# Layer 0's loop on one Trainium2 core: ScalarE copies the taps ahead of statistics and k, and GpSimd makes the differences of x one unit sooner, in three pieces around its ticks

## The chip, the cores and the metric

The kernel runs on one core of a Trainium2 chip. The metric is the device time of one launch in microseconds. TensorE (PE) multiplies matrices, VectorE (DVE) and ScalarE (ACT) work on tiles in SBUF and PSUM, GpSimd (POOL) on tiles in SBUF, and SyncE (SP) issues the DMAs. Each engine works through its own list of instructions in order, and this kernel writes that order out by hand.

## The reference, cut to what matters

The input x is 4 x 64 x 256 x 256 in float32. Layer 0 adds to x a convolutional block of its group norm, and layer 1 adds to that a block of two 3x3 convolutions with batch norms. The change is in layer 0:

```python
h = gelu(conv2d(gn(x), c1_w, 3x3) + c1_b)
h = c1x1(h, c2_w, c2_b)
xa, k = split(h, 2)
xs = conv2d(xa, sh_w, 1x3, groups=C) + sh_b      # the taps, across
xs = gelu(conv2d(xs, sv_w, 3x1, groups=C) + sv_b) # the taps, down
pooled = xs.mean(axis=(2, 3))                     # gate: weights of 3 experts
for (w1, w2, w3) in experts:
    out += mask * c1x1(c1x1(k, w2) * c1x1(xs, w1), w3)
x = x + c1x1(out, proj_w, proj_b)
```

## The kernel before, in words

**Units and slots.** Layer 0 cuts the four images into 64 units of 16 rows each (two halves of 8 rows on the two halves of the 128 partitions). `plan_front` (from L1023) lays the work of all units into slots. In slot u the engines do, side by side, the 3x3 convolution of unit u, the preparation of units u+1 and u+2, and the taps of units u-1 and u-2. `at_slot(u, pos, call)` puts a call at a position in the slot; positions run from 0 to about 9.2. All calls are sorted by slot and position and then issued under a manual schedule, so a position decides where the instructions of a call stand in each engine's own queue and nothing else: a call at 4.3 and one at 4.5 run at the same time if they are on different engines and no data binds them.

**The convolution** is done in a transformed domain along the rows (six products in place of the rows' taps). What goes into it is the tile `v` with six parts, of which there is one copy. GpSimd makes it out of a unit's ten rows, tile `x`:

- `x_four` (L522, ScalarE, one instruction at L526): four times some rows, into `x4`. One buffer.
- `x_differences` (L528, GpSimd, six instructions): two that finish `x4` (L532), then four that turn x in place into differences two rows apart (L535), each of which waits for the one before. `x_edges` (L510) puts the mean in place of a row beyond the image at the first and last unit of an image, one more instruction (L517), seven times in all.
- `x_scaled` (L537, ScalarE): twice some rows of the differences into `e2` (L540), and four times others in place (L542). It needs all the differences.
- `v_inner` (L551, GpSimd): v1 and v2 from x4 (L556, L557), v3 and v4 from the differences and e2 (L558, L559).
- `v_outer` (L561, GpSimd): v0 and v5 from the scaled differences (L563, L564).

TensorE reads v in `front_conv` (matmuls at L492): v1 and v2 at position 1, v3 and v4 at 1.3, v0 and v5 at 5. Each part of v can be written for unit u+1 only when these matmuls of unit u are through. ScalarE copies one half of each result (`front_copy`, tile `mc`, L594), VectorE combines them in PSUM (L599 to L618), and ScalarE takes the gelu into `h` (`front_h`, L626).

**The taps.** `front_taps_a` opens the one PSUM bank `ps_a` for one half of a unit's rows (24 records of 64x512); `front_taps_b` adds the rows at the edges (eight records of 64x256). Then ScalarE copies the bank, scaled, into t (`front_taps_i`, L666), VectorE adds the left and the right neighbour out of the bank (`front_taps_h`, L672 and L675, then L678 on t alone), and ScalarE takes the gelu into xs (`front_xs`, L694). The bank is free for the next half when L675 has read it. Each slot has two such halves: of unit u-2 at positions 2, 4, 4.15, 5.2, 5.3, and of unit u-1 at 7, 9, 9.1 and, in the slot after, 1.15 and 1.55.

**Ticks.** Between `front_taps_a` and `front_taps_b` stands `divide` (L483): GpSimd sets one column (`tick`, L485) when the last matmul issued before it is through, and the first matmul of the edge taps waits for that instruction. There are two in each slot, at 2.2 and 7.2. A tick is an instruction in GpSimd's queue like any other.

**What else ScalarE does.** `stats_piece` (L426, tile `xs_in`, L432) sums x plus a shift and then its squares for the next image's group norm, two instructions a piece. The plan gives slots 1 to 11 three pieces each (two in slot 11) and slots 12 to 43 two; slots 44 to 63 have none. In even slots `front_k` (L701) multiplies h with the experts' matrix for k into the bank `p` (L708), and ScalarE copies it (L716); in odd slots `front_q` and `front_low` do the like with xs, with VectorE reading the result.

**Output work** of an earlier image joins the loop from slot 19 on: TensorE's `ps_o` at positions 3 and 6 in the bank `p`, VectorE's L831 and L836, loads and stores on SP. The group norms' and the gate's small steps sit at fixed places, some with a table load on ScalarE ahead of `front_xs`.

After slot 63 the loop's last steps are put among the steps of layer 1 by a table (`TAIL`).

## Time and profile before

| What | us |
|---|---|
| Median of three runs | 3071.86 (3065.21 to 3072.45) |
| The profiled execution | 3069.24 |
| Its span, first to last instruction | 3067.4 |
| Busy: PE, DVE, ACT, POOL | 2372.5, 2458.7, 2054.9, 1675.0 |
| Granted TensorE clock, mean | 0.911 |

| Stretch of the loop, us | PE busy | DVE busy | ACT busy | POOL busy | DMA share |
|---|---|---|---|---|---|
| 97 to 467 | 316.14 | 260.12 | 312.89 | 294.62 | 0.61 |
| 467 to 928 | 421.27 | 377.24 | 342.45 | 337.45 | 0.94 |
| 928 to 1305 | 361.02 | 333.40 | 222.51 | 291.31 | 0.87 |

The profile shows one execution. A group's row gives the line, engine, operation and tiles (out <- in), and how often and how long it ran. A row of the timeline gives the start, the duration, the engine and line, and, in brackets, how long the engine had been idle before and what released it. A row of the waits gives the total, the number and the longest. TensorE's weight loads (PEld) are listed apart from its matmuls. The loop of layer 0 fills the first 43% or so of the span; layer 1's convolutions and the last pass over the output fill the rest.

### The profile page before, as it was taken

To read this page: it belongs to the slowest core of one execution; us is meant where nothing else is said; L and a number is where in the kernel's file an instruction comes from. 1 tells how busy PE (TensorE), PEld (TensorE's weight loads), DVE (VectorE), ACT (ScalarE), POOL (GpSimd) and SP (SyncE) were. 2 spreads that over 40 slices of the span, in tenths; PEclk is the share of its full clock that TensorE was granted. 3 is DMA by queue.
4 is the path that set the end of the run, shared out by engine and by line. 5 is a ranking of instruction groups with operands and counts; after the bars stand their busy time and mean duration, and the time that the engine had idled before them with its cause. 6 is when DMAs were issued, how large, how long until landed. Compare 5 with 4: busy or idle time off the path is not lost.

```text
span 3067.4 us, 53128 instructions
## 1 busy us (share of the span) xinstructions
PE 2372.5 (77%) x21576; PEld 1519.2 (50%) x21576; DVE 2458.7 (80%) x2793; ACT 2054.9 (67%) x2274; POOL 1675.0 (55%) x1210
## 2 busy tenths in 40 slices
PE   1888889998999999978889999998999999200000
PEld 1444445444444545545566666776888888200000
DVE  5567677888888988867788888988998999886665
ACT  6888877777776655556566767877888888433222
POOL 5877877777677877744345545645555555000000
PEclk9999999999999999999999999998999999655555
DMA  8664579999898989838889988765777764799999
GB/s 339 205 226 188 193 254 338 344 352 327 323 348 297 307 290 315 301 146 294 320 303 343 362 316 326 261 250 195 262 265 260 271 255 142 305 426 427 426 427 405
DMA packets 135573, 915.36 MB, mean 298 GB/s; under 512 B 14944, under 2 KB 15712, under 8 KB 40608
## 3 DMA queue, kind: packets, MB, share of 16 engines
q1 hardware_dynamic: 135328, 911.97, 79.6%
q8 instruction: 169, 2.77, 0.4%
q14 instruction: 76, 0.62, 0.1%
HBM read 573.74 MB, written 338.17 MB: 297 GB/s over the span
## 4 chain that ended last, share of the span: by engine, by line
PE 27%; DMA 18%; DVE 6%; issue 2%; ACT 1%; POOL 1%; SPq 0%; DVEq 0%; ACTq 0%; POOLq 0%
PE ps_h L295 17%; PE ps_h2m L295 6%; DMA y_end<-y_d 5%; DMA h<-h_d 4%; DMA out<-h 3%; DMA y<-in_xp 3%; PE ps_hm L295 3%; DMA xs_in<-xs_d 2%; DVE h L317 1%; PE ps_o L492 1%; DVE diff L352 1%; DVE odd L361 1%; DMA yn<-y_d 1%; DVE y L831 1%; DVE h L1398 1%
## 5 line engine op out<-in xcount | busy, mean ns | idle before, releaser
L295 PE MATMUL ps_h<-diff,w_q 128*128 128x512 f32 x3072 | 754.6, 400 | 11.5 <-DVE h L317 11.5
L295 PEld LDWEIGHTS ps_h<-diff,w_q 128*128 128x128 f32 x3072 | 579.2, 190 | 183.7 <-issue 29.9
L492 PE MATMUL ps_c<-v,us 64*64 64x256 f32 x9216 | 541.2, 383 | 37.4 <-DVE ps_c L612 32.7
L342 POOL TENSOR_TENSOR d<-yn 128x1024 f32<-128x1024 f32 x128 | 355.9, 2801 | 319.1 <-DMA yn<-y_d 182.1
L492 PE MATMUL ps_a<-h,av 64*64 64x512 f32 x4080 | 400.5, 506 | 88.6 <-DVE t L675 69.2
L492 PEld LDWEIGHTS ps_c<-v,us 64*64 64x64 f32 x9216 | 362.9, 135 | 189.0 <-DVE ps_c L612 40.7
L342 POOL TENSOR_TENSOR d<-h 128x1024 f32<-128x1024 f32 x127 | 312.1, 2480 | 194.6 <-DVE diff L350 133.4
L317 DVE SCALAR_TENSOR_TENSOR h<-ps_h,scale_w,m 128x1024 f32<-128x1024 f32 x256 | 323.5, 1279 | 63.5 <-PE ps_h L295 47.3
L492 PEld LDWEIGHTS ps_a<-h,av 64*64 64x64 f32 x4080 | 160.3, 136 | 369.4 <-issue 260.6
L535 POOL TENSOR_TENSOR x<-x 128x512 f32<-128x512 f32 x256 | 328.2, 1282 | 15.5
L672 DVE SCALAR_TENSOR_TENSOR t<-ps_a,m,t 128x1020 f32<-128x1020 f32 x128 | 163.6, 1278 | 201.4 <-ACT t L666 200.7
L1397 ACT ACTIVATE v<-y_end,shift,gn 128x2048 f32<-128x2048 f32 x64 | 133.8, 2092 | 279.2 <-DMA y_end<-y_d 244.0
L381 ACT ACTIVATE junk<-h,less_h 128x2048 bf16<-128x2048 f32 (+3 forms) x133 | 256.0, 1925 | 11.1 <-DVE h L317 10.9
L1398 DVE SCALAR_TENSOR_TENSOR h<-h,ss,v 128x2048 f32<-128x2048 f32 x64 | 149.8, 2350 | 120.2 <-ACT v L1397 120.2
L831 DVE SCALAR_TENSOR_TENSOR y<-ps_o,ob,y 128x1024 f32<-128x1024 f32 x128 | 163.9, 1280 | 90.6 <-PE ps_o L492 43.1
L666 ACT ACTIVATE t<-ps_a,tap_bias,m 128x1024 f32<-128x1024 f32 x128 | 153.8, 1201 | 99.3 <-PE ps_a L492 98.8
L295 PE MATMUL ps_h2m<-odd,w_q 128*128 128x512 f32 x768 | 193.2, 400 | 8.2 <-DVE odd L361 4.4
L694 ACT ACTIVATE xs<-t 128x1024 f32<-128x1024 f32 x128 | 134.5, 1051 | 94.0 <-issue 72.7
L295 PE MATMUL ps_hm<-odd,w_q 128*128 128x512 f32 x768 | 194.2, 402 | 3.7 <-DVE t L675 3.0
L352 DVE SCALAR_TENSOR_TENSOR diff<-d,gn,diff 128x1024 fp32r<-128x1024 f32 x128 | 190.3, 1517 | 4.9 <-ACT diff L345 4.9
L345 ACT ACTIVATE diff<-d 128x1024 fp32r<-128x1024 f32 x128 | 135.1, 1055 | 83.6 <-POOL d L342 82.3
L626 ACT ACTIVATE h<-ps_c,c1b 128x1024 f32<-128x1024 f32 x128 | 135.6, 1110 | 73.3 <-DVE ps_c L618 69.7
(226 smaller groups left out, 4348.0 us busy)
## 6 DMA issues: line engine op xcount, KB each, us to landing
h_d<-h SPq DMA_DIRECT2D x114, 1024.0 KB
x<-in_xc SPq DMA_DIRECT2D x64, 1280.0 KB
h<-h_d SPq DMA_DIRECT2D x64, 1152.0 KB
yn<-y_d SPq DMA_DIRECT2D x60, 1152.0 KB
xs_in<-in_xp SPq DMA_DIRECT2D x64, 1024.0 KB
xs_d<-xs SPq DMA_DIRECT2D x128, 512.0 KB
xs_in<-xs_d SPq DMA_DIRECT2D x64, 1024.0 KB
y<-in_xp SPq DMA_DIRECT2D x64, 1024.0 KB
```

The costliest lines, as they stand in the source:

```text
L295: nc.tensor.matmul(ps, wq[w][:, kind, kx, :], t[:, rows, kx : kx + W], start=(j == 0), stop=(j == len(terms) - 1))
L317: nc.vector.scalar_tensor_tensor(h.rearrange("p (e k) w -> p e (k w)", e=2), ps.rearrange("p e k w -> p e (k w)"), w_scale[w], m.unsqueeze ...
L342: engine.tensor_tensor(raw.rearrange("p (g r) w -> p g r w", g=2), *pair, ALU.subtract)
L352: nc.vector.scalar_tensor_tensor(lower, raw, scale, upper.bitcast(F32), ALU.mult, ALU.subtract)
L381: nc.scalar.activation(junk[rows, 0:n], flat(h), AF.Square, bias=less[name][rows], accum_out=total)
L492: last[:] = [nc.tensor.matmul(ps[o, at_out[0] : at_out[1], :], w[i], rhs[i], **flags)]
L535: nc.gpsimd.tensor_tensor(x[:, r : r + 2], x[:, r + 2 : r + 4], x[:, r : r + 2], ALU.subtract)
L626: nc.scalar.activation(hs[u][:, :, rows, :], ps, AF.Gelu, bias=c1_bias[u // NCH])
L666: nc.scalar.activation(flat(t), flat(ps), AF.Identity, bias=tap_bias, scale=sh[:, 1:2])
L672: nc.vector.scalar_tensor_tensor(t[:, :, 1:W], ps[:, :, 0 : W - 1], sh[:, 0:1], t[:, :, 1:W], ALU.mult, ALU.add)
L831: nc.vector.scalar_tensor_tensor(y, ps.rearrange("p x s w -> p x (s w)"), out_bias[b], y, ALU.add, ALU.add)
L1398: nc.vector.scalar_tensor_tensor(h, h, ss2[:, 0:1], v, ALU.mult, ALU.add)
```

## The change

ScalarE: the statistics move. Of the pieces in the first half of a slot the sum goes from position 1.12 to 1.6, behind the copies of the convolution, `x_scaled` and `front_xs`; the squares stay at 4.4. Of the pieces in the second half the sum goes from 6.5, behind `front_h`, to 5.4, ahead of it, and the squares from 7.15 to 9.15, behind the copy of the taps (9.1). The copy of k's result leaves `front_k` (position 8) and becomes `front_k_out` at 9.2, also behind the copy of the taps.

GpSimd: `x_differences` is split into `x_fourths` (the two on x4) and `x_seconds` (two of the four on x at a time). In place of all six for unit u+1 at 0.5, behind the second tick of the slot before, stand, for unit u+2: the fourths at 4.5 (behind `x_four` at 4.3, which doesn't move), two of the seconds at 6.6 and two at 7.3, with the second tick (7.2) between. `v_inner` is split too: v1, v2 and v3 at 1.9, ahead of the first tick (2.2), and v4 at 2.3 behind it. Only slot 0 still makes all differences of unit 1 at 0.5. GpSimd's order in a slot is so:

| Before | After |
|---|---|
| fourths, four seconds (u+1) | v1, v2, v3 (u+1) |
| tick one | tick one |
| v1, v2, v3, v4 (u+1) | v4 (u+1) |
| v0, v5 (u+1) | fourths (u+2) |
| tick two | v0, v5 (u+1) |
| | two seconds (u+2) |
| | tick two |
| | two seconds (u+2) |

No arithmetic is added or left out, and no DMA, matmul or VectorE instruction changes its place in its queue.

```diff
+    def x_fourths(u):
+        x4 = x4s[u]
         for j in (1, 2):
             nc.gpsimd.tensor_tensor(x4[:, j - 1], x_rows(u, j + 2), x4[:, j - 1], ALU.subtract)
-        x_edges(u)
-        for r in range(0, 8, 2):
+
+    def x_seconds(u, rows):
+        x = xt[u]
+        if 0 in rows:
+            x_edges(u)
+        for r in rows:
             nc.gpsimd.tensor_tensor(x[:, r : r + 2], x[:, r + 2 : r + 4], x[:, r : r + 2], ALU.subtract)
...
-    def v_inner(u):
+    def v_inner(u, part=None):
+        if part != 1:
...
+            nc.gpsimd.tensor_tensor(at_v(3), x_rows(u, 2), e2s[u], ALU.add)
+        if part != 0:
+            nc.gpsimd.tensor_tensor(at_v(4), x_rows(u, 2), e2s.pop(u), ALU.subtract)
...
+        ps_k[b, j] = ps
...
+    def front_k_out(b, j):
+        ps = ps_k.pop((b, j))
         k_sb[b, j] = work.tile([P, 2, GF], F32, tag="k", name=f"k_{b}_{j}", bufs=1)
         nc.scalar.activation(flat(k_sb[b, j]), ps.rearrange("p s f -> p (s f)"), AF.Identity, bias=k_bias)
...
             if u + 1 <= last:
-                at_slot(u, 0.5, x_differences, u + 1)
+                if u == 0:
+                    at_slot(u, 0.5, x_differences, 1)
                 at_slot(u, 1.5, x_scaled, u + 1)
-                at_slot(u, 2.3, v_inner, u + 1)
+                at_slot(u, 1.9, v_inner, u + 1, 0)
+                at_slot(u, 2.3, v_inner, u + 1, 1)
                 at_slot(u, 5.5, v_outer, u + 1)
             if u + 2 <= last:
                 at_slot(u, 4.3, x_four, u + 2)
+                at_slot(u, 4.5, x_fourths, u + 2)
+                at_slot(u, 6.6, x_seconds, u + 2, (0, 2))
+                at_slot(u, 7.3, x_seconds, u + 2, (4, 6))
...
                 at_slot(u, 8, front_k, *divmod(j, NOCT // 4))
+                at_slot(u, 9.2, front_k_out, *divmod(j, NOCT // 4))
...
-                    at_slot(int(s), ((1.12, 4.4) if first else (6.5, 7.15))[part], stats_piece, b, 2 * k + i, part)
+                    at_slot(int(s), ((1.6, 4.4) if first else (5.4, 9.15))[part], stats_piece, b, 2 * k + i, part)
```

The table `TAIL` gets one more entry, for the copy of k's result in slot 64: (3, 13.35).

## The prediction

> **What bounds the kernel now.** I read the page (busy shares), then the waits of 140 to 1540 us, then the timeline of two slots. The change touches only layer 0's loop: 64 slots, from about 64 to 1340 us, some 20 us each. Its waits (who waited for whom: total us, times, longest):

> ```profile
> POOL tick L485 <- PE ps_a L492: 298.0, 109, 10.0
> DVE t L672 <- ACT t L666: 181.8, 89, 8.6
> PE ps_a L492 <- DVE t L675: 68.8, 41, 7.6
> PEld ps_a L492 <- POOL tick L485: 11.9, 17, 0.8
> ```

> GpSimd mostly waits for TensorE at its ticks and hardly ever the other way round; TensorE's largest wait is for L675, the second reader of the single tap bank. A slot with statistics shows why (start us, duration, engine, line):

> ```profile
> 827.17 0.66 PE L492 MATMUL ps_a<-h,av 64*64 64x256 f32 x8
> 827.92 1.15 ACT L432 ACTIVATE xs_in<-xs_in,shift 128x1024 f32<-128x1024 f32 x1
> 829.19 1.06 ACT L432 ACTIVATE xs_in<-xs_in 128x1024 f32<-128x1024 f32 x1
> 830.24 1.19 ACT L666 ACTIVATE t<-ps_a,tap_bias,m 128x1024 f32<-128x1024 f32 x1
> 832.78 1.28 DVE L675 SCALAR_TENSOR_TENSOR t<-ps_a,m,t 128x1020 f32<-128x1020 f32 x1
> 834.21 2.38 PE L492 MATMUL ps_a<-h,av 64*64 64x512 f32 x24 [1.19 <-ACT e L540]
> 838.09 0.64 PE L492 MATMUL ps_a<-h,av 64*64 64x256 f32 x8
> 838.88 1.21 ACT L666 ACTIVATE t<-ps_a,tap_bias,m 128x1024 f32<-128x1024 f32 x1 [2.54 <-PE ps_a L492]
> 839.98 1.05 ACT L526 ACTIVATE x<-x 128x1024 f32<-128x1024 f32 x1
> ```

> I cut every slot at its two groups of edge taps (the eight 64x256 matmuls on ps_a, each behind a tick): B, position 9, here at 827.17; A, position 4, ending here at 838.73. Read from the timeline, B to the end of A takes 11.56 us in such slots and 12.53 with k; the end of A to the next B takes 8.28. Without statistics TensorE has no gap, and the slot is 18.96:

> ```profile
> 1239.31 0.61 PE L492 MATMUL ps_a<-h,av 64*64 64x256 f32 x8
> 1242.90 1.29 POOL L563 TENSOR_TENSOR v<-x 128x512 f32<-128x512 f32 x1
> 1244.15 1.27 POOL L564 TENSOR_TENSOR v<-x 128x512 f32<-128x512 f32 x1
> 1247.12 0.10 POOL L485 MEMSET tick<- 128x1 f32 x1 [1.70 <-PE ps_a L492]
> 1247.24 2.53 POOL L532 TENSOR_TENSOR x<-x,x 128x512 f32<-128x512 f32 x2
> 1248.78 0.66 PE L492 MATMUL ps_a<-h,av 64*64 64x256 f32 x8
> 1249.72 5.33 POOL L535 TENSOR_TENSOR x<-x 128x512 f32<-128x512 f32 x4
> ```

> The second tick stands right behind v_outer here, so it was ready 1.7 us before TensorE let it go, and all six differences of x ran after it. From B to B the three stretches took: 97.11 to 427.06, 17 slots without output work, 330.0 us; 427.06 to 950.86, 25 with output and statistics, 523.8; 950.86 to 1305.65, 18 with output alone, 354.8. Sum 1208.5.

> [...] the tick starts when its predecessors and PE are done. [...] Here the spans are 1.28, the spacing 1.25 (1242.90 to 1244.15), and 1.35 where one difference waits for the one before ((5.33-1.28)/3). [...] the trace's 1.25 is used. [...] the trace has 1.05 (square) and 1.14 (identity).

> **The change part by part.**

> *ScalarE, position 9.* The statistics pair (2.32 us, 827.92 to 830.24) and k's copy (L716, about 1.0) leave the front of L666. L666 then starts right after B's end, at B+0.8, L675 ends at about B+4.7, and conv's two groups hold TensorE until B+5.7. The wait is gone: B to A falls to 10.14, as in the slots without statistics. Gain 1.42 and 2.39 a slot. Identity at 5.4 fits the gap ahead of gelu (1.51 idle before L626 in such slots). Square and k's copy now end at B+4.1, ahead of the second mc copy (B+5.9): nothing. k's bank is next written by output work at about B+8: nothing.

> *ScalarE, position 1.6.* The identity moves from 1.12 to behind xs. Spacings of the slot at 827.17: mc at B+5.93, e 6.42, x 7.08, xs 8.04, so the identity starts at 9.10 and, with 1.13 each, lets L666 (position 4.15) go at B+10.23 (one) or 11.36 (two, in four early slots). With output work A ends at B+10.14, L666 could go at 10.28 anyway: nothing. Without output work A ends at about B+9.12, and it costs 1.0 or 2.1.

> *GpSimd, first half.* v1 to v3 go ahead of tick one. v1 waits for conv's first group (B+3.3), v3 for e (B+7.05), so tick one is at about B+8.4; TensorE wants it at B+8.2 without output work, a microsecond later with it. Cost 0.2 or nothing.

> *GpSimd, second half: the large term.* Queued ahead of tick two are now: two fourths (L532), waiting for ScalarE's L526, then two v_outer, then two of the four seconds. Behind the tick stands TensorE's B. L526 is behind L666, which waits for A. So, from the end of A: L666 at 0.14, L526 at 1.25 (1.11 later), its end 2.30, fourths 2.36, v_outer 4.84, seconds 7.33, their end 7.33+1.35+1.28 = 9.96, tick and semaphore 0.10: B at A+10.06. Before, 8.28 in most slots and 8.65 to 8.86 in the last ones. Cost 1.2 to 1.8 in every one of 60 slots. The cover was TensorE's own 8.3 us; the chain is longer than that. The latency ScalarE to GpSimd (0.06) is the least known: 0.0 to 0.2. In 7 slots x_edges (L517, 0.92, spacing 0.9) joins this chain.

> *Not moved:* no DMA issue; x's loads keep their place on SP's queue, and v_outer, later by some 2.4 us, still frees the ring tile before the load that takes it (position 0 of the next slot).

> The sum. Period = start of L666 + 9.92.
> Stretch 1: four slots of 11.36+9.92 = 21.28, 85.1; thirteen of 20.15, 262.0; edges 1.8; two slots with table loads ahead of xs (2.9 us of ScalarE at about 338 us), now in the chain, 6: 354.9, against 330.0, +24.9.
> Stretch 2: 25 of 10.14+10.06 = 20.20, 505.0; edges 1.8; three slots with table loads 6; stalls of the gate and of throttled stretches that stay, read as the excess of B to A over 12.5 (4.3 and three of 1.7) 9.4: 522.2, against 523.8, -1.6.
> Stretch 3: 18 of 20.20, 363.6; edges 2.7; table loads 6; stalls that stay 5: 377.3, against 354.8, +22.5.
> Prologue: seconds of unit 2 move ahead of tick one of slot 1: +1.5.
> Total +47. The profiled execution took 3069.24 (span 3067.4), so 3116 on its own time; the median shown is 2.6 higher, and I leave it at 3116, since with TensorE idle more, some of the half-clock stretches in the loop may not come.

> **Rivals.**
> 1. The tick comes free (faster). Then only the removed wait counts: 25 slots of 1.9, 48, and five early ones (B to A 10.9 to 13.6, down to 9.3) 16: 3005. This needs the path from L526's end to tick two to fit in 8.28-2.30 = 6.0 us; six operations at 1.25 are 7.5, and 298 us of waiting at ticks, which speaks for it, lies in places that the new order can't use, since L526 comes late. Against it: that is queue order.
> 2. A wash. The chain as computed, but nothing else: table loads, edges and double identities hidden, stalls gone. 17 of 19.18 and 43 of 20.20 are 1194.7, 14 less than before: at best 3055, with half of the extras 3080. For it: TensorE's new idle time can absorb DVE's delays. Against it: the identity and the table loads are on ScalarE ahead of L666, and the chain has no slack.
> 3. More is late: the identities at 5.4 push gelu beyond B in early slots[...]. 0.2 us on each of six operations is 60 x 1.2 = 72: 3150 and more. The spacings hardly vary in the trace.

> **Chances.** Forecast 0.72 (3090 to 3140), wash 0.15 (3055 to 3090), tick free 0.05, more late 0.08. A measurement can tell about 0.3%, 9 us, from no change. Range 3085 to 3140: the latency's ends are -4 and +8, the kept stalls and table loads (33) may halve or grow by a quarter. Faster 0.06, same 0.09, slower 0.85.

> **What would show it.** After: the waits lose PE ps_a <- DVE L675 and have PE ps_a <- POOL tick as TensorE's largest in the loop, near 1.3 to 1.9 us a slot; GpSimd's wait at the second tick is gone, and it waits for L526 instead; B to A is 10.1 and A to B 10.1 in slots with output, which shows as one period, near 20.2, with and without statistics. It is wrong if B follows A by 8.3, or if L532 starts before L666.

## The result, and the profile after

| What | Before | After |
|---|---|---|
| Median of four runs, us | 3068.53 (3060.53 to 3072.45) | 3145.88 (3144.6 to 3146.63) |
| Ratio, 95% interval | | 1.0255 (1.0231 to 1.0279) |
| Span of the profiled execution | 3067.4 | 3144.3 |
| Mean granted clock | 0.911 | 0.91 |

The change costs 77 us. The forecast had the direction and the mechanism, and +47; its range ended at 3140. In the changed kernel lines above 526 have moved: e is L549, taps copy L677, the two readers L683 and L686, k's copy L733, the seconds L540, the fourths L532.

The waits of the changed kernel, 140 to 1620 us (total us, times, longest):

```profile
DVE t L683 <- ACT t L677: 190.8, 111, 6.6
POOL x L532 <- ACT x L526: 182.9, 58, 5.7
PE ps_a L492 <- POOL tick L485: 105.3, 72, 2.8
PE ps_a L492 <- DVE t L686: 57.2, 25, 7.6
POOL tick L485 <- PE ps_a L492: 41.8, 7, 10.0
```

The third and the last row have changed places against the kernel before: GpSimd's tick hardly ever waits for TensorE now, TensorE waits for the tick 72 times. L686, the second reader of the bank, isn't gone: in rows with statistics and output (440 to 960) TensorE waits 13.3 us for it (27.4 before, 430 to 950), but in the rows without output, ahead of 440, still 30.3 (26.5 before), there between A and B. The POOL row with L526 is new and says what the tick is late for: the fourths wait for it 58 times. One slot shows the chain (start us, duration, engine, line; idle time before in brackets):

```profile
1206.51 0.61 PE L492 MATMUL ps_a<-h,av 64*64 64x256 f32 x8
1207.25 1.21 ACT L677 ACTIVATE t<-ps_a,tap_bias,m 128x1024 f32<-128x1024 f32 x1 [1.10 <-PE ps_a L492]
1208.36 1.05 ACT L526 ACTIVATE x<-x 128x1024 f32<-128x1024 f32 x1
1209.48 2.50 POOL L532 TENSOR_TENSOR x<-x,x 128x512 f32<-128x512 f32 x2 [2.78 <-ACT x L526]
1211.95 1.30 POOL L574 TENSOR_TENSOR v<-x 128x512 f32<-128x512 f32 x1
1213.20 1.28 POOL L575 TENSOR_TENSOR v<-x 128x512 f32<-128x512 f32 x1
1214.43 2.63 POOL L540 TENSOR_TENSOR x<-x 128x512 f32<-128x512 f32 x2
1217.00 0.10 POOL L485 MEMSET tick<- 128x1 f32 x1
1217.16 0.66 PE L492 MATMUL ps_a<-h,av 64*64 64x256 f32 x8 [1.69 <-POOL tick L485]
```

A ends at 1207.12 and B starts at 1217.16, 10.04 later; in between GpSimd runs without a gap from the end of L526 on, and TensorE stands still for 1.69.

From here on a row is the piece of the loop from one B to the next, numbered 1 to 63; rows 1 to 17, 18 to 42 and 43 to 60 are the three stretches of the forecast. Row 1 begins at 100.07 (97.11 before).

| Rows | Before | Forecast | After |
|---|---|---|---|
| 1 to 17 | 330.0 | 354.9 | 364.5 |
| 18 to 42 | 523.8 | 522.2 | 532.5 |
| 43 to 60 | 354.8 | 377.3 | 382.6 |
| 61 to 63 | 65.1 | not forecast | 66.9 |
| Start of row 1 | 97.11 | +1.5 | +2.96 |

A regular row with output is 10.14 + 10.04 = 20.18 (forecast 20.20), one without output 9.20 + 10.88 = 20.08 (20.15), one with two identities 21.20 (21.28). So the chain was right to 0.1 us, and what is missing, 25 us in rows 1 to 60, lies in the irregular rows.

### The profile page after: what moved, and what is told of

The parts are those of the page before. It is cut to its first block, busy times and chain, and to the rows that moved or that the text cites. A ratio compares the mean times of both kernels' runs of the same rounds, so it can differ in the third digit from the quotient of the medians.

```text
span 3144.3 us, 53038 instructions
## 1 busy us (share of the span) xinstructions
PE 2372.0 (75%) x21576; PEld 1507.4 (48%) x21576; DVE 2500.6 (80%) x2793; ACT 2055.5 (65%) x2274; POOL 1667.4 (53%) x1210
## 3 DMA queue, kind: packets, MB, share of 16 engines
q8 instruction: 169, 2.77, 0.4%
## 4 chain that ended last, share of the span: by engine, by line
PE 27%; DMA 18%; DVE 5%; issue 2%; ACT 1%; SPq 0%; POOL 0%; DVEq 0%; ACTq 0%
PE ps_h L295 17%; PE ps_h2m L295 5%; DMA y_end<-y_d 4%; DMA out<-h 4%; DMA h<-h_d 4%; PE ps_hm L295 3%; DMA y<-in_xp 2%; DMA xs_in<-xs_d 2%; PE ps_o L492 1%; DVE h L317 1%; DVE diff L352 1%; DVE odd L361 1%; DVE y L848 1%; DMA y_d<-y 1%; DVE h L1422 0%
## 5 line engine op out<-in xcount | busy, mean ns | idle before, releaser
L492 PE MATMUL ps_c<-v,us 64*64 64x256 f32 x9216 | 547.3, 387 | 22.7 <-DVE ps_c L623 18.3
L492 PE MATMUL ps_a<-h,av 64*64 64x512 f32 x4080 | 399.4, 506 | 173.4 <-POOL tick L485 110.1
L492 PEld LDWEIGHTS ps_c<-v,us 64*64 64x64 f32 x9216 | 364.3, 137 | 176.9 <-DVE ps_c L623 20.7
L492 PEld LDWEIGHTS ps_a<-h,av 64*64 64x64 f32 x4080 | 155.2, 136 | 454.0 <-issue 211.7
L540 POOL TENSOR_TENSOR x<-x 128x512 f32<-128x512 f32 x256 | 328.5, 1283 | 13.3
L683 DVE SCALAR_TENSOR_TENSOR t<-ps_a,m,t 128x1020 f32<-128x1020 f32 x128 | 163.7, 1279 | 213.8 <-ACT t L677 213.8
L532 POOL TENSOR_TENSOR x<-x,x 128x512 f32<-128x512 f32 x128 | 160.4, 1275 | 211.0 <-ACT x L526 211.0
L677 ACT ACTIVATE t<-ps_a,tap_bias,m 128x1024 f32<-128x1024 f32 x128 | 153.9, 1202 | 113.5 <-PE ps_a L492 113.4
```

Of the source, the lines that this page charges most:

```text
L492: last[:] = [nc.tensor.matmul(ps[o, at_out[0] : at_out[1], :], w[i], rhs[i], **flags)]
L532: nc.gpsimd.tensor_tensor(x4[:, j - 1], x_rows(u, j + 2), x4[:, j - 1], ALU.subtract)
L540: nc.gpsimd.tensor_tensor(x[:, r : r + 2], x[:, r + 2 : r + 4], x[:, r : r + 2], ALU.subtract)
L677: nc.scalar.activation(flat(t), flat(ps), AF.Identity, bias=tap_bias, scale=sh[:, 1:2])
L683: nc.vector.scalar_tensor_tensor(t[:, :, 1:W], ps[:, :, 0 : W - 1], sh[:, 0:1], t[:, :, 1:W], ALU.mult, ALU.add)
```

## The experiments

Each is compared with the kernel before, run beside it on the same chip (medians of 3069.7 to 3071.2). Four texts name theories by letters: T is the forecast's chain to tick two, S blames ScalarE's new order, V the move of v1 to v3 ahead of tick one.

### Which part of the change costs

ScalarE's part alone: GpSimd's calls are put back.

```diff
-                if u == 0:
-                    at_slot(u, 0.5, x_differences, 1)
+                at_slot(u, 0.5, x_differences, u + 1)
...
-                at_slot(u, 1.9, v_inner, u + 1, 0)
-                at_slot(u, 2.3, v_inner, u + 1, 1)
+                at_slot(u, 2.3, v_inner, u + 1)
...
-                at_slot(u, 4.5, x_fourths, u + 2)
-                at_slot(u, 6.6, x_seconds, u + 2, (0, 2))
-                at_slot(u, 7.3, x_seconds, u + 2, (4, 6))
```

> The changed kernel with GpSimd's order put back (all six differences of unit u+1 behind tick two, v1 to v4 behind tick one); ScalarE's moves alone are kept. Theory T (the chain ScalarE L526, two fourths, two v_outer, two seconds, tick two holds TensorE's edge taps B): the end of A to B is 8.3 to 8.9 again, B to the end of A stays 10.14 with output work, period 18.5 to 19.0 in all slots with output; about 3020 (3005 to 3040), faster than before. Rival S (ScalarE's new order is what costs: the identity ahead of the taps' copy at 4.15, squares and k ahead of the copies of the convolution): near 3146. Rival V (v1 to v3 ahead of tick one delay that tick): as T.

Measured 3056.92, ratio 0.9956 (0.9943 to 0.9969). GpSimd's part alone (ScalarE's 1.6, 5.4, 9.15 and 9.2 put back to 1.12, 6.5, 7.15 and 8.01):

> The changed kernel with ScalarE's order put back (statistics at 1.12, 4.4, 6.5 and 7.15, k's copy right behind its matmuls); GpSimd's moves alone are kept. T: A to B 10.04 in every slot, and B to A as before (11.56 and 12.53 with statistics and output), so 21.6 and 22.6 there: about 3175 (3160 to 3195), slower than the whole change. S: 3069. V: 3146.

Measured 3137.95, ratio 1.0220 (1.0190 to 1.0251). So GpSimd's part is the loss, +68, and ScalarE's alone is a gain of 13, less than T gave it. Added up the parts give 55, not 77: together they cost 22 more than apart. Both misses teach something. Alone, GpSimd's part should have kept TensorE's wait for the second reader of the bank, B to A 11.56 or 12.53; it is 10.23, and 11.24 with k. While TensorE stands 1.7 us at tick two, ScalarE is already at the statistics pair: in row 23 it begins 0.58 before B (552.45 against 553.03), where it began 0.75 behind B in the kernel before (827.92 against 827.17), so the taps copy comes 1.3 sooner behind B. The two legs of a slot aren't independent: of the 1.42 and 2.39 that ScalarE's part saves, GpSimd's part has taken 1.3 already. And ScalarE's part alone reached the 10.14 + 8.28 to 8.85 of the working, but only where the loads of y for the output work don't hold it. In its waits, 440 to 940 us, stands

```profile
DVE y L848 <- DMA y<-in_xp: 25.5, 7, 5.0
```

against 1.0, 2 times, in the kernel before and 2.9, 3 times, in the changed one. Rows 22, 24, 26, 28 and 32 take 20.6 to 22.6 there. (The profiled execution was the longest of twenty, 3070.75 against a median of 3056.92, so the usual one may wait less.) The DMA engines are 0.93 busy in that stretch with 340 GB/s (0.93 and 335 before): with faster slots y's load is issued late, since the store that frees its buffer ends late (in the fastest version below, SP waits for that store 26.8 us in 560 to 650). Rival 1 of the forecast, the free tick at 3005, left this limit out: below, a version in which the tick does come free waits 24.1 us for y (430 to 950) and takes 3073.89.

### Is it the chain to tick two

All four seconds behind the tick (6.6 becomes 7.25), and all four ahead of it (7.3 joins 6.6):

```diff
-                at_slot(u, 6.6, x_seconds, u + 2, (0, 2))
+                at_slot(u, 7.25, x_seconds, u + 2, (0, 2))
```

```diff
-                at_slot(u, 6.6, x_seconds, u + 2, (0, 2))
-                at_slot(u, 7.3, x_seconds, u + 2, (4, 6))
+                at_slot(u, 6.6, x_seconds, u + 2, (0, 2, 4, 6))
```

> The changed kernel with all four seconds behind tick two (6.6 becomes 7.25). T: two operations of 1.35 leave the chain, which is then 10.04 - 2.7 = 7.35, under TensorE's own 8.3: A to B 8.3 to 8.9, tick two no longer waited for. Tick one comes at B+9.2, at no cost with output work, some 1.0 without: about 3035 (3015 to 3060). S and V: 3146, since neither's order is touched.

Measured 3077.25, ratio 1.0025 (1.0013 to 1.0037). A to B is back at 8.27 to 8.8, as T has it; the 42 us missing to 3035 are again y's loads (23.2 us in its waits of 430 to 950) and the irregular rows.

> The changed kernel with all four seconds ahead of tick two. T: two operations of 1.35 join the chain: A to B 12.74 in place of 10.04, 60 slots of 2.70: 3146 + 162 = 3308 (3295 to 3320). S and V: 3146, no more than 10 above it.

Measured 3390.75, ratio 1.1051 (1.1013 to 1.1090). A to B is 12.73 to 12.76, the 10.04 + 2.70 of the working; but B to A, which nothing touched, rose from 10.14 to 11.4 to 13, 77 us in sum over rows 1 to 60. Its TensorE shows how:

```profile
1151.70 1.92 PE L741 MATMUL ps_q<-xs,m 128*32 128x512 f32 x16
1158.03 1.13 PE L492 MATMUL ps_a<-h,av 64*64 64x256 f32 x8 [4.40 <-POOL tick L485]
1158.93 7.78 PE L492 MATMUL ps_c<-v,us 64*64 64x256 f32 x96
```

The same eight matmuls take 0.66, and the 96 of the convolution 5.36, where TensorE waited 1.7 us. From 1157.02 to 1163.85 the granted clock of this kernel is 0.50, half rate. To test whether the gap does it, the next kernel keeps the chain and fills the gap: TensorE repeats k's and q's matmuls.

```diff
-        for t in range(2):
+        for t in range(5):
...
-                        wk[half, s, t, :],
+                        wk[half, s, t % 2, :],
...
-        for s in range(2):
+        for s, n in ((0, 0), (1, 0), (0, 1), (1, 1), (0, 2)):
...
```

> The kernel with all four seconds ahead of the second tick (A to B 12.75, TensorE waits 4.4 us at the tick), in which TensorE repeats the matmuls of k and of q one and a half times more (k and q are sums of 2.5 times the products: their values are not the reference's), so that some 2.9 us of the 4.4 us are filled with matmuls; what waits for the tick is the same. That kernel took 3390.8, where 3308 was worked out, because B to A rose from 10.14 to 11.4 to 13. Theory that a long gap of TensorE is followed by matmuls at half rate: with a gap of 1.5 us B to A is back at 10.14 to 10.3, taps behind the tick take 0.66 instead of 1.13, and the time is 3310 (3300 to 3325). Rival (the slower matmuls come from something else, such as the transfers or a throttle that more matmuls would make worse): B to A stays at 11.4 to 13, 3390 or more. Rival 2 (the matmuls added are themselves in the way): A to B above 12.8.

Measured 3308.61, ratio 1.0767 (1.0748 to 1.0787). With more work on TensorE it is 82 us faster:

```profile
1103.31 4.50 PE L741 MATMUL ps_q<-xs,m 128*32 128x512 f32 x40
1109.64 0.66 PE L492 MATMUL ps_a<-h,av 64*64 64x256 f32 x8 [1.84 <-POOL tick L485]
1110.13 5.36 PE L492 MATMUL ps_c<-v,us 64*64 64x256 f32 x96
```

Behind the gap of 1.84 the eight take 0.66 and the 96 take 5.36 again, and B to A is back at 10.14. So in this chain the half rate came with TensorE's own gap of 4.4: that was shown by shortening the gap and leaving the wait's cause in place (A to B of regular rows stays at 12.73 to 12.82).

### Where the missing 25 us are

After row 28 in the changed kernel:

```profile
688.47 1.93 PE L741 MATMUL ps_q<-xs,m 128*32 128x512 f32 x16
693.23 0.66 PE L492 MATMUL ps_a<-h,av 64*64 64x256 f32 x8 [2.84 <-POOL tick L485]
693.71 4.46 PE L492 MATMUL ps_c<-v,us 64*64 64x256 f32 x48
```

Row 28 has an x_edges in the chain, so the gap is 2.84 instead of 1.7, and the 48 matmuls take 4.46 where 2.77 is usual; from 694.59 to 698.00 the granted clock is 0.50. In the traces of the eight kernels here whose tick two is late (430 to 1300 us) half rate followed one of 239 gaps of 1.0 to 2.74 us before edge taps (a gap of 2.67), 8 of 11 gaps of 2.80 to 2.99, and all 32 of 3.2 and more; the text below counts fewer kernels and lacks the one at 2.67. The next kernel moves the edges to where GpSimd idles for L526:

```diff
-        if 0 in rows:
-            x_edges(u)
...
+                at_slot(u, 4.25, x_edges, u + 2)
                 at_slot(u, 4.5, x_fourths, u + 2)
```

> The changed kernel with x_edges (GpSimd, seven slots) at 4.25, ahead of the fourths, where GpSimd idles for L526, instead of inside the seconds ahead of tick two; nothing else moves. My theory has two parts. The edges' own time leaves the chain: A to B of rows 12, 28, 44 and 60 falls from 11.2 to 10.05, and of rows 13, 29 and 45 by 0.9. And TensorE's gap at the tick that follows rows 12, 28 and 44 falls from 2.84 to 1.7 us, below the 2.8 us from which the traces so far show half rate (none of 168 gaps of 1.0 to 2.74 us, 7 of 9 of 2.8 to 3.0, all of 29 of 4.2 and more): B to A of rows 13, 29 and 45 falls by 1.7, to 9.7, 10.6 and 10.6. Saved 4.6 + 2.7 + 5.1 = 12.4; 3133.5 (3131 to 3137). Rival (half rate comes by chance or from something else in these rows): 7, 3139, and B to A of rows 13, 29 and 45 stays at 11.4, 12.3 and 12.3.

Measured 3134.54, ratio 1.0204 (1.0190 to 1.0218). The same place in it (there the k and q lines have moved by two):

```profile
681.26 1.92 PE L739 MATMUL ps_q<-xs,m 128*32 128x512 f32 x16
684.92 0.66 PE L492 MATMUL ps_a<-h,av 64*64 64x256 f32 x8 [1.73 <-POOL tick L485]
685.40 2.77 PE L492 MATMUL ps_c<-v,us 64*64 64x256 f32 x48
```

B to A of rows 13, 29 and 45 fell from 11.35, 12.30 and 12.30 to 9.67, 10.61 and 10.61, as worked out; A to B of rows 12, 28, 44 and 60 fell by 1.06 to 1.09, of rows 29 and 45 by 1.0. But the length of the gap alone doesn't decide: in the kernel with the identity back at 1.12 (below), the gaps ahead of rows 29 and 45 are still 2.83 and 2.84, no half rate follows, and B to A is 10.61 there too. What else the traces show of such gaps is in the last section.

The second kind of stall, also from row 28 (TensorE's 128x1 matmul of the group norm and what releases it):

```profile
672.41 1.05 ACT L432 ACTIVATE xs_in<-xs_in 128x1024 f32<-128x1024 f32 x1
673.45 1.10 ACT L733 ACTIVATE k<-ps_k,k_bias 128x1024 f32<-128x1024 f32 x1
674.61 0.38 PE L266 MATMUL ps_m_x<-mv_x,m 128*128 128x1 f32 x2 [0.83 <-ACT k L733]
```

The small matmul takes the one bank p, which k's copy still has to read. It did so in row 28 of the kernel before:

```profile
636.16 0.38 PE L266 MATMUL ps_m_x<-mv_x,m 128*128 128x1 f32 x2 [0.94 <-ACT k L716]
```

There B to A was the regular 12.54 all the same; the wait for L675 covered it. With the copy ahead of the square (its entry in `TAIL` moves likewise):

```diff
-                at_slot(u, 9.2, front_k_out, *divmod(j, NOCT // 4))
+                at_slot(u, 9.12, front_k_out, *divmod(j, NOCT // 4))
```

> The changed kernel with one order number altered: k's copy on ScalarE at 9.12, ahead of the square of the statistics (9.15), instead of 9.2 behind it; nothing else moves. My theory: in rows 12, 14, 28, 30, 44 and 46 TensorE waits 0.5 to 1.3 us between the two convolution groups because the 128x1 matmul of the group norm takes the same single PSUM bank that k's copy has still to read. One square (1.24 us) sooner, the copy lets it go at once: B to A of rows 28 and 30 falls from 11.51 to 10.2 to 10.4, of rows 12 and 14 from 10.5 to 9.3; regular slots stay at 20.18; the sum is -5 us, 3141 (3137 to 3145). Rival (the matmul waits for DVE's statistics, or the square is wanted sooner than k): B to A of rows 28 and 30 stays at 11.5, or mc's copy is pushed, 3146 and more.

Measured 3142.81, ratio 1.0229 (1.0210 to 1.0247). B to A of rows 28 and 30 fell to 10.61, of rows 12 and 14 to 9.67 and 9.62: 0.9 in four rows, 3.6 us. (Row 29 fell by 1.7: its gap was 2.42 and no half rate followed.) The 0.47 that stay are the small matmul itself; rows 44 and 46, without statistics, had only these and didn't change. The 3 us between the medians are of the size of the runs' spread; the rows carry the verdict.

The third kind is the gate's chain on VectorE, in row 34 of the changed kernel:

```profile
809.01 1.20 DVE L784 TENSOR_SCALAR keep<-keep 128x3 f32<-128x3 f32 x1
810.32 1.88 DVE L287 BATCH_NORM_AGGREGATE mv_y<-st_y 128x2 f32<-128x384 f32 x1
812.35 0.56 PE L266 MATMUL ps_m_y<-mv_y,m 128*128 128x1 f32 x2 [4.00 <-DVE pick L791]
812.84 5.08 PE L492 MATMUL ps_c<-v,us 64*64 64x256 f32 x48
```

TensorE waits 4.00 us for VectorE's tiny steps and then runs 48 matmuls at half rate (5.08 where 2.77 is usual; the granted clock is 0.50 from 810.64 to 817.47). Row 34 has this in both kernels, B to A 17.02 before and 17.12 after. Against the regular 12.53 that was an excess of 4.5, against the new 10.14 it is 7.0. To see whether the same work is worth more after the change, the gate's comparison (seven small instructions) is left out of both kernels:

```diff
-        beat = stat.tile([P, 6], F32, tag="beat", name=f"beat_{b}")
...
-        nc.vector.tensor_tensor(keep, g[:, 0:3], keep, ALU.mult)
-        yield
+        keep = g[:, 0:3]
+        yield
```

> The changed kernel without the pairwise comparison in the gate (beat and keep, seven small DVE instructions of some 3.9 us that stand ahead of L683 in rows 18, 34 and 50; the gate's weights go on unthresholded, so this part of the computation is left out). My theory: a stall that TensorE keeps is worth its whole excess over the new, shorter B to A of 10.14. Row 34 falls from 17.12 to between 10.2 and 11, row 50 from 16.27 to between 10.2 and 11, row 18 from 14.20 to between 10.2 and 11; saved 16 (13 to 18), 3130. Rival, the reading of the forecast: the stall is worth its excess over 12.5, as in the kernel before; saved 10 or less, 3136 or more.

> The kernel before with the same seven instructions left out. My theory: in rows of statistics and output the stall lies in part under TensorE's wait for L675, so the same removal is worth less here: row 34 falls from 17.02 to 12.5 (-4.5, against -6 to -7 in the changed kernel), row 18 stays near 12.2 (0, against -3 to -4), row 50, which has no wait for L675, from 16.03 to 10.3 (-5.7, as there); saved 10 (8 to 11), 3060. Rival (the stall is no more hidden here than there): saved the same 16, 3054.

| Row | Before | Without | Saved | After | Without | Saved |
|---|---|---|---|---|---|---|
| 18 | 20.46 | 19.37 | 1.1 | 24.25 | 20.18 | 4.1 |
| 34 | 25.31 | 23.77 | 1.5 | 27.18 | 22.69 | 4.5 |
| 50 | 24.31 | 22.83 | 1.5 | 26.32 | 23.39 | 2.9 |

Medians 3063.48 (ratio 0.9977, 0.9969 to 0.9985) and 3130.89 (1.0192, 1.0174 to 1.0211): 7 saved before the change and 15 after it, in these three rows 4.1 and 11.5. The contrast is as my theory has it, the single sizes aren't: rows 34 and 50 kept 12.6 and 12.8 from B to A, since the aggregate and the steps behind it stay on VectorE, and row 50, which had no wait for L675 to hide under, saved 2.9 against 1.5 all the same; its cause stays open.

Part of the contrast is the clock, and these two runs don't separate it. In rows 18, 34 and 50 the changed kernel had one, two and one half-rate spells of 3.41 us, and without the comparison none; the kernel before had none, two and one, and without it none, one and none. So the theory rests on two rows more than on the sums. Row 34 itself hardly moved with the change, 17.02 to 17.12, while the regular rows around it fell from 12.53 to 10.14. And where row 18 has no half rate (the runs with k's copy sooner and with the edges early), its B to A is 12.00 and 12.09, 1.9 over the regular 10.14, against 12.17 and no excess over 12.5 before.

### Why the chain is late, and a version that is faster

The forecast's other cost was the identity behind xs. With it back at 1.12:

```diff
-                    at_slot(int(s), ((1.6, 4.4) if first else (5.4, 9.15))[part], stats_piece, b, 2 * k + i, part)
+                    at_slot(int(s), ((1.12, 4.4) if first else (5.4, 9.15))[part], stats_piece, b, 2 * k + i, part)
```

> The changed kernel with the identity of a slot's first statistics piece back at 1.12 (ahead of mc's copy) instead of 1.6 (behind xs, ahead of the taps copy L677). My theory: as it stood in the forecast, the identity behind xs costs 1.0 us in each slot without output (A to B 10.88 to 10.05, less what B to A gives: rows 5 to 17 fall from 20.08 to 19.2) and 2 us in the four slots with two of them (21.2 to 19.2), and nothing in slots with output: -20 to -25 us, 3122 (3116 to 3130). Rival: L677 isn't what GpSimd waits for there (v4 and v_outer are): rows 5 to 17 stay at 20.1, 3146.

Measured 3127.92, ratio 1.0179 (1.0162 to 1.0197): rows 5, 9 and 15 fell to 19.24, rows 1 to 4 by 6.2 in all and rows 5 to 17 by 7.3; regular rows with output didn't change. On top of this kernel, x_four goes ahead of the taps copy, while GpSimd's whole new order stays:

```diff
-                at_slot(u, 4.3, x_four, u + 2)
+                at_slot(u, 4.1, x_four, u + 2)
```

> The changed kernel with the first identity back at 1.12 (3127.9 that way) and, new here, x_four (L526) at 4.1, ahead of the taps copy L677, instead of 4.3 behind it. All of GpSimd's new order stays: fourths, v_outer and two seconds ahead of the second tick. My theory: it is L526, held behind L677 and so behind A, that makes the chain to tick two late. Ahead of L677 it ends by A+0.1 to 0.5 instead of A+2.3, the tick is ready at A+7.7 to 8.3, and A to B falls from 10.05 to TensorE's own 8.3 to 8.9; stretch 3 falls from 381 to 345 to 355, stretch 2 from 529 to 500 to 512 (held there by the loads of y, as in the run with ScalarE's part alone), stretch 1 to 330 or less; 3040 (3025 to 3055). Rival 1 (six differences of 1.25 are too long wherever L526 stands, or v4 behind the first tick holds the fourths): A to B stays over 9.5, 3100 or more. Rival 2 (L677 and DVE behind it come late by a square): B to A or A to B grow by 1, 3075 to 3130.

Measured 3073.89, ratio 1.0004 (0.9992 to 1.0016). One slot of it:

```profile
1147.64 1.04 ACT L526 ACTIVATE x<-x 128x1024 f32<-128x1024 f32 x1
1148.09 0.61 PE L492 MATMUL ps_a<-h,av 64*64 64x256 f32 x8
1148.75 2.52 POOL L532 TENSOR_TENSOR x<-x,x 128x512 f32<-128x512 f32 x2 [0.47 <-ACT x L526]
1148.83 1.21 ACT L677 ACTIVATE t<-ps_a,tap_bias,m 128x1024 f32<-128x1024 f32 x1 [0.15 <-PE ps_a L492]
1156.29 0.10 POOL L485 MEMSET tick<- 128x1 f32 x1
1156.98 0.66 PE L492 MATMUL ps_a<-h,av 64*64 64x256 f32 x8
```

L526 starts before A ends, the tick is done at A+7.7 (0.6 before B), and A to B is 8.27 to 8.32 in 25 of the 43 rows with output, 8.95 to 8.97 in the regular ones without; sixteen others have 9.7 to 12.7, and VectorE waits 24.1 us for y's loads from 430 to 950. One queue position of one ScalarE instruction undoes 54 us: the six GpSimd operations are affordable, what they waited for was not. The time I gave, 3040, was missed by 34: stretch 2 came to 509.7, as given, but stretch 3 to 361.2 instead of 345 to 355 and rows 1 to 17 to 335.8. Rows 44, 45 and 51 have 12.4 to 12.7 from A to B; I haven't taken these apart.

Last, ScalarE's part without GpSimd's, with the identity at 1.12 and k's copy at 9.12:

> ScalarE's part of the change alone (GpSimd's order as before the change; 3056.9), with two order numbers altered: the first identity back at 1.12, k's copy at 9.12. My theory: the parts are not all bad; the taps copy ahead of the statistics pair pays where TensorE waits for DVE, and the identity behind xs costs. Rows 1 to 4 fall from 21.8 to 17.5 or 18 (-15), rows 5 to 17 by 0.4 to 1 each (-8), the four stalls behind k -4: 3030 (3018 to 3042), faster than both kernels. Rival: with the identity at 1.12 mc's copy and DVE behind it come late, and rows 1 to 17 gain nothing or B to A rises to 10 to 11 there: 3050 to 3070.

Measured 3033.02, ratio 0.9868 (0.9849 to 0.9887), 37.6 us faster than before. In the profiled execution, the longest of four (3042.31), rows 1 to 4 take 72.5 (72.1 before), rows 5 to 17 245.4 (257.8 before), rows 18 to 42 508.2 (523.8), rows 43 to 60 352.1 (354.8). It is the best of the versions here; VectorE still waits 30.4 us for y's loads from 430 to 950.

## Why the prediction was right, and where it failed

- **B to A 10.14, and the wait for the second reader gone:** right. That this gain is ScalarE's part's own was wrong in what it implied: with GpSimd's part in, 1.3 of the 1.42 and 2.39 comes anyway (10.23 and 11.24 without ScalarE's).
- **"the waits lose PE ps_a <- DVE L675":** half right; the wait at B to A went, the one between A and B in rows without output stayed, as it had to, with L675's work unchanged.
- **Identity behind xs, 1.0 or 2.1:** right for one, 20.08 against 19.24; for two it was less, 21.2 against 20.0 in rows 2 and 4.
- **v1 to v3 ahead of tick one, 0.2 or nothing:** right; B to A in rows without output is 9.20, against 8.91 where only ScalarE's part is in.
- **The chain A+0.14, 1.25, 2.36, ... 10.06:** right, 10.04. "six operations at 1.25 are 7.5" and "L526 comes late" were the decisive sentences; the run with x_four sooner shows that the second of them was the cause.
- **Where the sum failed: "stalls of the gate and of throttled stretches that stay, read as the excess of B to A over 12.5".** These terms were 9.4 and 5, 14.4 in all. Measured, B to A exceeds its regular values (9.20, 10.14) by 5.6 in rows 5 to 17, 16.9 in 18 to 42 and 10.2 in 43 to 60: 32.7. In the kernel before, TensorE's wait for L675 and a small stall overlapped, so the excess over 12.5 showed only what stuck out: row 18 showed none there, and rows 28 to 30 0.0 to 0.3. With the wait gone, these came out in full: the gate's chain, with the half rate behind it, 17.2 (rows 18, 34, 50), the bank p behind k's copy 3.6, the small matmuls' own 0.47 in some fourteen rows about 7. "k's bank is next written by output work at about B+8: nothing" was the false reading behind the second: the group norm's small matmul wants it at B+3.3. The last 5 are half rate in rows 13, 29 and 45 (0.50 for 3.41 us from 353.25, 694.59 and 1039.33). The forecast's "three of 1.7" were half rate too, in rows 20, 32 and 42 (granted clock 0.50 for 3.41 us from 475.51, 724.68 and 936.31); these ran at full rate after the change, and the three others came in their place.
- **Smaller misses:** table loads, edges and the like on A to B 30.4 against 24.3; rows 1 to 4 +2.6 (rows 1 and 3 have 1.7 and 1.2 extra); the prologue +1.5; rows 61 to 63 +1.8, which the sum left out. With the 18.3 of the stalls these make 30, less 2 for regular rows that were a little shorter than worked out: 28 of the 30 between the profiled execution's +76.9 and the forecast's +47.
- **"the half-clock stretches in the loop may not come" with more idle time:** half right. In rows 5 to 60 the kernel before had eleven half-rate spells of 3.41 us and the changed one ten: those of rows 6, 8, 10, 20, 32 and 42 are gone, those behind the new gaps came. But rows 1 to 4 had none before and have six after.
- **Rival 3** had the right size, 3150, and the wrong reasons: the spacings of GpSimd's operations stayed at 1.25 (1211.95 to 1213.20), and in the stretch of identities at 5.4 B to A and A to B are the forecast's.

## What to carry to other kernels

A wait that is removed has been hiding others: read every stall that shares a leg with it against the length that the leg will have, not against the length that it has. When work is queued ahead of a synchronising instruction, ask first when its latest operand is made, and by which queue: here moving the producer by one place was worth more than the order of the six operations behind it. And a gap on TensorE had a second price here beyond its own length: behind one of 4.40 the 96 matmuls took 7.78 instead of 5.36. Length alone didn't tell which gap has it: ahead of row 45 half rate followed one of 2.83 and not one of 2.84.

## What the runs showed of the hardware that I had not expected

With this agrees that the same gap costs something in one place and nothing in another. Two gaps of the kernel before, alike in length and cause, ahead of the same 24 matmuls:

```profile
475.39 4.08 PE L492 MATMUL ps_a<-h,av 64*64 64x512 f32 x24 [2.16 <-DVE t L675]
557.78 2.38 PE L492 MATMUL ps_a<-h,av 64*64 64x512 f32 x24 [2.16 <-DVE t L675]
```

The first lies in a window that was busy 0.37 (472.10 to 475.51), and the next, to 478.92, runs at 0.50; the second is split between windows of 0.72 and 0.66. In the changed kernel the gap of 2.83 ahead of row 45 lies in a window of 0.17; with the identity back at 1.12 the one of 2.84 is split, 0.67 and 0.49, and costs nothing. With the grid agrees, too, that the taps at 693.23 still took 0.66: the window at half rate began at 694.59. No run here moves a gap along the grid and changes nothing else, so that its place is the cause was not shown.

Filling a gap of 4.4 us with 2.6 us of needless matmuls made a kernel 82 us faster.
